# Two bursts of weight spreading in every third slice of an attention and convolution kernel

## The chip, the cores and the metric

The kernel runs on one core of a Trainium2 chip. The metric is the device time of one execution in microseconds, lower is better. TensorE (PE) does the matmuls, VectorE (DVE) elementwise work and reductions, ScalarE (ACT) activations and copies, GpSimd (POOL) elementwise work between SBUF tiles, and SyncE (SP) issues most DMAs.

## The reference

Two layers with a residual each, on x of 16 images of 56 x 56 pixels and 384 channels, all in float32:

```
x = x + attention(group_norm(x))      # layer 0
x = x + depthwise_conv(group_norm(x)) # layer 1

attention: qkv = x @ w_qkv.T; three groups of 128 channels with dilations 1, 2, 3
  for each group, 4 heads of 32 channels, each pixel attends to its 3 x 3 dilated neighbours:
    attn = softmax over 9 of (q . k_neighbour) * 32 ** -0.5
    out  = sum over 9 of attn * v_neighbour
  y = concat(out) @ w_proj.T + b_proj
depthwise_conv: 3 x 3, one filter a channel, weights replaced by their signs (after a clip)
group_norm: 32 groups of 12 channels, over all pixels of an image, no scale or shift
```

## The kernel before

Channels lie on the partitions. The work is cut into 112 chunks (index m): 7 chunks of 8 rows (448 pixels, PX) for each of 16 images. Three planners put the pieces of each chunk on a common clock of slices with `at(when, order, piece)`: `plan_a` turns the input and takes its statistics, `plan_b` is the attention, `plan_c` the convolution. A chunk starts every 9 slices (STEP), so in the steady state each run of nine slices holds the same mixture of pieces of several chunks; the texts call it a round. At the end the pieces are emitted sorted by slice, and within a slice by the order constants of line 833. The framework's scheduler may then still move an instruction past others when it expects it to be ready earlier or later; the buffers of the pools and all waits are derived from the program. Each engine takes its own instructions strictly in the resulting order.

Of `plan_b`, with t0 = 9m, these pieces matter:

- `query(g)` (L483, slices t0-1, t0+2, t0+5): nine 128x448 projections give q of group g in the one bank of `ps_q`.
- `score(i)`, i = 0 to 8 (L509, slice t0+i; i = 3g + ky): VectorE multiplies q with three shifted views of k into a tile t of 3 x 448 (L517). The nine scores of a pixel and head are sums over 32 channels. They are made by matmuls of t with a selection matrix `sel` that is 32 columns wide (L502, tile ps), collected in `ready` and issued in bursts by `score_rounds`: at i = 2 and 5 eight of them, at i = 8 eleven. Each float32 matmul is two instructions in the profile: 16 and 22.
- `softmax_1` to `softmax_5` and `turn_weights` (slices t0+9 to t0+12): transposes (pt_s, L537), maximum, exponent, sum and division on VectorE and ScalarE (L540 to L548), a split of each weight into three bfloat16 terms (ScalarE L556, GpSimd L560, L564, L565), and a DMA that transposes them into aT (L570, on SyncE's queue).
- `weigh(i)`, i = 0 to 8 (L574, slices t0+14+i): three bfloat16 matmuls with 24 rows each (tile pb_a, L583) spread the weights of three neighbours over the 32 channels of their heads into the three banks of `ps_bc`, which has one buffer. The texts call these three a burst, and burst i is that of weigh(i). VectorE multiplies pb_a with three shifted views of v into w (L590). GpSimd adds the second and third w of a group to the first (L598) and then sums the three neighbours into y (L601, L602).
- `out_project(j)` (L608, slices t0+24+j): po from y0, y1, y2 (L616), residual and statistics on VectorE (L619, L622).
- `k_or_v` (L468): pkv (L464), copied by ScalarE (L474), with halo rows copied by DMAs (L478, L479).

Of `plan_c`: three loads make z from x1d (L684), ScalarE normalises z (L697) and zg (L740) and multiplies nine taps for the last group of channels (L769), GpSimd sums them (L776, L782, L785), and `convolve(j)` (L705) does 24 matmul instructions of 96 rows and 32 columns (pc, L711). In the rounds at an image's start the convolution is one slice later. `turn(s)` (pt_o, L792) turns results for the output. Once an image `group_norm` makes statistics by small steps on TensorE, VectorE and GpSimd (L309 to L382).

Most PSUM tiles (pt_x, pkv, po, pt_s, pt_o, pc) share the three buffers of `ps_mt`, so each waits until the tile three before it is read out. `in_one_go` (L289) keeps the matmuls of a burst together.

What fixes the place of the two kinds of bursts is

```
if i % 3 == 2:
    score_rounds(3 if i == 8 else 2)                   
at(t0 + 14 + i, WEIGH, lambda i=i: weigh(i))           
SOFTMAX, SCORE, STATISTICS, CONVOLVE, WEIGH, QUERY, ...
```

Of the kernel before, what the change touches and what calls it, by code (L numbers as in the profile page):

```python
# [35 lines left out]
def dilated_attention_then_binary_conv(  # L36
# [39 lines left out]
    def place(p):  # L76

        g, o = divmod(p, NTAP)
        return NG * o + g
# [201 lines left out]
    def rows(ap):  # L281
        return ap.rearrange("p (r w) -> p r w", w=W)

    def three(t, d, ky):

        tw = t[:, ky * d : ky * d + ROWS, 0:W]
        return bass.AP(tw.tensor, tw.offset, [tw.ap[0], (d, 3), *tw.ap[1:]])

    def in_one_go(matmuls):  # L289

        matmuls[0]()
        with tc.high_priority():
            for m in matmuls[1:]:
                tc.keep_in_program_order(m())
# [97 lines left out]
    def at(when, order, piece):  # L392

        pieces.setdefault((when, order), []).append(piece)
# [51 lines left out]
    def plan_b(m, t0):  # L446
# [44 lines left out]
        def score_rounds(rounds):  # L491

            burst = ready[: rounds * NQ]
            del ready[: rounds * NQ]
            if "ps" not in had:
                had["ps"] = ps_s.tile([P, 512], F32, tag="s", name="ps")

            def add(p, tk):
                j, i = p % NQ, p // NQ
                s0 = SEL0 - 4 * i  # L500
                issued[j] += 1
                return nc.tensor.matmul(  # L502
                    had["ps"][32 * j : 32 * j + 32, :PX], sel[:, s0 : s0 + 32], tk,
                    start=(issued[j] == 1), stop=(issued[j] == len(range(j, NG * NTAP, NQ))),
                )

            in_one_go([lambda a=a: add(*a) for a in burst[-1:] + burst[:-1]])

        def score(i):  # L509

            g, ky = divmod(i, 3)
            d = DIL[g]
            qg = rows(had["q"][:, :PX])
            q3 = bass.AP(qg.tensor, qg.offset, [qg.ap[0], (0, 3), *qg.ap[1:]])
            k3 = three(kv[0][g][m % K_SLOTS], d, ky)
            t = t_p.tile([P, 3, PX], F32, tag="t", name="t")
            nc.vector.tensor_tensor(t.rearrange("p k (r w) -> p k r w", w=W), q3, k3, ALU.mult)  # L517
            ready.extend((i * 3 + kx, t[:, kx, :]) for kx in range(3))
            if i % 3 == 2:
                score_rounds(3 if i == 8 else 2)  # L520

        GH = NG * HEADS
        weights = ew.rearrange("p (s v) -> p s v", s=NSUB)[:, :, :NR]
# [50 lines left out]
        def weigh(i):  # L574

            g, ky = divmod(i, 3)
            pb = ps_bc.tile([P, 3, 512], F32, tag="bc", name="pb_a")

            def copy(kx):
                v = place(3 * i + kx)  # L580
                lo = 32 * (v // 2 % 4)
                rows_of = slice(lo, lo + 2 * TERMS * HEADS)
                return nc.tensor.matmul(  # L583
                    pb[:, kx, :PX].rearrange("p (s n) -> p s n", s=NSUB), spread[rows_of, v % 2, :],
                    had["a"][rows_of, :, v // 8, :], start=True, stop=True
                )

            in_one_go([lambda kx=kx: copy(kx) for kx in (2, 0, 1)])
            w = w_p.tile([P, 3, PX], F32, tag="w", name="w")
            nc.vector.tensor_tensor(  # L590
                w.rearrange("p k (r w) -> p k r w", w=W),
                pb[:, :, :PX].rearrange("p k (r w) -> p k r w", w=W), three(kv[1][g][m % V_SLOTS], DIL[g], ky), ALU.mult,
            )
            if ky == 0:
                had["w0"] = w
                return
            w0 = had["w0"]
            nc.gpsimd.tensor_tensor(w0, w0, w, ALU.add)  # L598
            if ky == 2:
                had[f"y{g}"] = y = y_p.tile([P, PX], F32, tag="y", name="y")  # L600
                nc.gpsimd.tensor_tensor(y, w0[:, 0], w0[:, 1], ALU.add)  # L601
                nc.gpsimd.tensor_tensor(y, y, w0[:, 2], ALU.add)  # L602
# [29 lines left out]
            at(t0 - 1 + 3 * g, QUERY, lambda g=g: query(g))  # L632
        for i in range(9):
            at(t0 + i, SCORE, lambda i=i: score(i))
        at(t0 + 9, SOFTMAX, softmax_1)
        at(t0 + 10, SOFTMAX, softmax_2)
        at(t0 + 11, SOFTMAX, softmax_3)
# [1 line left out]
        at(t0 + 12, SOFTMAX, softmax_5)  # L639
        at(t0 + 12, LOADS, turn_weights)  # L640
        for i in range(9):
            at(t0 + 14 + i, WEIGH, lambda i=i: weigh(i))
        at(t0 + 20, LOADS, load_residual)
        for j in range(NG):
            at(t0 + 24 + j, PROJECT, lambda j=j: out_project(j))
# [184 lines left out]
        for s in range(NSUB):  # L830
            at(t0 + 9 + s, STAGE_C, lambda s=s: turn(s))

    SOFTMAX, SCORE, STATISTICS, CONVOLVE, WEIGH, QUERY, SPREAD, QKV, PROJECT, STAGE_A, STAGE_C, NORM, LOADS = range(13)

    STAT_ORDER = (STATISTICS, SPREAD, SPREAD, SPREAD, STATISTICS, SPREAD)
    STEP = 9
# [45 lines left out]
    for m in range(N):  # L882
        plan_a(m, start_a(m))
        plan_b(m, STEP * m)
        plan_c(m, STEP * (m + 10))
# [31 lines left out]
```

## Time and profile before

| | |
|---|---|
| median of 3 runs | 5253.52 us (5253.09 to 5254.31) |
| span of the profiled execution | 5259.5 us |
| granted TensorE clock | full in nearly all of the span |
| HBM traffic | 466 MB read, 231 MB written |

The page gives the busy time of each engine; the timeline lists instructions in order of time, runs of equal ones merged, with start, length and, in brackets, the idle time of the engine just before and what ended it. Names read out<-in with buffer numbers left out, then the shapes. A float32 matmul has 128x448 in its row and stands twice. A round of nine slices is found by the score sums x22, which come once in it. The queue of SyncE is listed as SPq: its rows are issues, not transfers.

### The profile page before, as it was taken

To read this page: it belongs to the slowest core of one execution; us is meant where nothing else is said; L and a number is where in the kernel's file an instruction comes from. 1 tells how busy PE (TensorE), PEld (TensorE's weight loads), DVE (VectorE), ACT (ScalarE), POOL (GpSimd) and SP (SyncE) were. 2 spreads that over 40 slices of the span, in tenths; PEclk is the share of its full clock that TensorE was granted. 3 is DMA by queue.
4 is the path that set the end of the run, shared out by engine and by line. 5 is a ranking of instruction groups with operands and counts; after the bars stand their busy time and mean duration, and the time that the engine had idled before them with its cause. 6 is when DMAs were issued, how large, how long until landed. Compare 5 with 4: busy or idle time off the path is not lost. (4 is left out here: it accounts for less than half of the span.)

```text
span 5259.5 us, 75515 instructions
## 1 busy us (share of the span) xinstructions
PE 5106.2 (97%) x26885; PEld 2327.2 (44%) x26885; DVE 4188.3 (80%) x4125; ACT 2313.4 (44%) x4077; POOL 4256.5 (81%) x2950
## 2 busy tenths in 40 slices
PE   7999999999999999999999999999999999999976
PEld 4444444444444444444444444444444444444423
DVE  4887888888888888888888878888888888878764
ACT  3223444444444444445444444444445444444443
POOL 2667888888888888888888788888888888898881
PEclk9999999999999999999999999999999999999987
DMA  6434556556555655565665566556565555554545
GB/s 195 126 113 109 165 162 169 158 160 167 156 164 164 170 164 159 163 167 164 161 161 165 151 170 166 160 165 165 165 164 164 161 159 165 141 139 135 136 134 157
DMA packets 811630, 825.62 MB, mean 157 GB/s; under 512 B 360307, under 2 KB 801014, under 8 KB 811254
## 3 DMA queue, kind: packets, MB, share of 16 engines
q1 hardware_dynamic: 803270, 808.79, 56.4%
q10 hardware_dynamic: 7984, 12.00, 0.7%
q8 instruction: 213, 3.49, 0.3%
q14 instruction: 163, 1.34, 0.1%
HBM read 466.41 MB, written 231.21 MB: 133 GB/s over the span
## 5 line engine op out<-in xcount | busy, mean ns | idle before, releaser
L598 POOL TENSOR_TENSOR w<-w 128x1344 f32<-128x1344 f32 x672 | 2075.4, 3088 | 457.0 <-DVE w L590 437.3
L590 DVE TENSOR_TENSOR w<-pb_a,v 128x1344 f32<-128x1344 f32 x1008 | 1554.8, 1542 | 241.3 <-PE pb_a L583 187.6
L517 DVE TENSOR_TENSOR t<-pq,k 128x1344 f32<-128x1344 f32 x1008 | 1536.7, 1551 | 228.7 <-PE pq L464 221.7
L464 PE MATMUL pkv<-xn,wqkvT 128*128 128x448 f32 x3924 | 1566.2, 548 | 0.4 <-DVE xr L619 0.4
L464 PEld LDWEIGHTS pkv<-xn,wqkvT 128*128 128x128 f32 x3924 | 717.5, 190 | 669.8 <-issue 643.4
L616 PE MATMUL po<-y,wprojT 128*128 128x448 f32 x2016 | 838.5, 552 | 56.8 <-POOL y L602 36.1
L697 ACT ACTIVATE z<-z,mrz 96x448 f32<-96x448 f32 x840 | 578.4, 751 | 676.6 <-DMA z<-x1d 407.4
L464 PE MATMUL pq<-xn,wqkvT 128*128 128x448 f32 x1962 | 833.9, 559 | 0.0
L776 POOL TENSOR_TENSOR m<-m 128x1344 f32<-128x1344 f32 x210 | 640.1, 3048 | 151.8 <-ACT m L769 147.6
L502 PE MATMUL ps<-t,sel 128*32 128x448 f32 x6048 | 658.4, 544 | 6.2 <-DVE t L517 5.3
L769 ACT ACTIVATE m<-zg,ktap 128x448 f32<-128x448 f32 x945 | 555.6, 659 | 16.5 <-POOL m L776 6.8
L616 PEld LDWEIGHTS po<-y,wprojT 128*128 128x128 f32 x2016 | 377.4, 192 | 417.8 <-issue 336.5
L711 PE MATMUL pc<-z,kdiag 96*32 96x440 f32 (+1 forms) x5040 | 514.0, 541 | 6.5 <-POOL z L699 4.4
L464 PEld LDWEIGHTS pq<-xn,wqkvT 128*128 128x128 f32 x1962 | 344.3, 189 | 318.1 <-issue 318.1
L619 DVE SCALAR_TENSOR_TENSOR xr<-po,bias,xr 128x448 f32<-128x448 f32 x336 | 228.6, 680 | 235.9 <-PE po L616 231.9
L602 POOL TENSOR_TENSOR y<-y,w 128x448 f32<-128x448 f32 x336 | 381.5, 1136 | 16.3
L601 POOL TENSOR_TENSOR y<-w 128x448 f32<-128x448 f32 x336 | 381.7, 1136 | 13.7
L474 ACT COPY v<-pkv 128x448 f32<-128x448 f32 x336 | 176.3, 525 | 483.8 <-PE pkv L464 466.1
L583 PE MATMUL pb_a<-aT,spread 24*128 24x448 bf16 x3024 | 368.4, 359 | 21.2 <-DMA aT<-e 10.9
L718 DVE TENSOR_TENSOR x<-pc,x 128x448 f32<-128x448 f32 x224 | 138.5, 618 | 272.1 <-PE pc L711 269.2
L474 ACT COPY k<-pkv 128x448 f32<-128x448 f32 x336 | 178.9, 532 | 377.7 <-PE pkv L464 377.7
L583 PEld LDWEIGHTS <-spread 24*128 24x128 bf16 x3024 | 98.3, 91 | 510.3 <-issue 489.2
(132 smaller groups left out, 4280.4 us busy)
## 6 DMA issues: line engine op xcount, KB each, us to landing
z<-x1d SPq DMA_DIRECT2D x570, 224.0 KB, 3.9
xr<-xd SPq DMA_DIRECT2D x112, 672.0 KB, 4.2
x1d<-xr SPq DMA_DIRECT2D x112, 672.0 KB, 3.2
xn<-xd SPq DMA_DIRECT2D x109, 672.0 KB, 4.6
xin<-in_x_dram SPq DMA_DIRECT2D x105, 672.0 KB, 7.5
xd<-xa SPq DMA_DIRECT2D x315, 224.0 KB, 3.4
out_dram<-osb SPq DMA_DIRECT2D x420, 168.0 KB, 3.5
x<-x1d SPq DMA_DIRECT2D x112, 448.0 KB, 8.3
```

Of the source, the lines that this page charges most:

```text
L464: nc.tensor.matmul(dst[:, :PX], wqkvT[:, cc, o0 : o0 + P], had["xn"][:, cc, :], start=(cc == 0), stop=(cc == NG - 1))
L502: return nc.tensor.matmul(had["ps"][32 * j : 32 * j + 32, :PX], sel[:, s0 : s0 + 32], tk, start=(issued[j] == 1), stop=(issued[j] == len(r ...
L517: nc.vector.tensor_tensor(t.rearrange("p k (r w) -> p k r w", w=W), q3, k3, ALU.mult)
L583: return nc.tensor.matmul(pb[:, kx, :PX].rearrange("p (s n) -> p s n", s=NSUB), spread[rows_of, v % 2, :], had["a"][rows_of, :, v // 8, :] ...
L590: nc.vector.tensor_tensor(w.rearrange("p k (r w) -> p k r w", w=W), pb[:, :, :PX].rearrange("p k (r w) -> p k r w", w=W), three(kv[1][g][m ...
L598: nc.gpsimd.tensor_tensor(w0, w0, w, ALU.add)
L601: nc.gpsimd.tensor_tensor(y, w0[:, 0], w0[:, 1], ALU.add)
L616: nc.tensor.matmul(po[:, :PX], wprojT[:, g, j * P : (j + 1) * P], had[f"y{g}"], start=(g == 0), stop=(g == NG - 1))
L697: nc.scalar.activation(z, z, AF.Identity, bias=mrz[:, j, q, 0:1], scale=mrz[:, j, q, 1:2])
L711: return nc.tensor.matmul(pcr[q * HD : (q + 1) * HD, :, lo:hi], kdiag[:, kx, j * NQ + q, :], rows(set_of(j, q))[:, :, lo + kx - 1 : hi + k ...
L769: nc.scalar.activation(rows(t[:, kx]), zp[:, ky : ky + ROWS, kx : kx + W], AF.Copy, scale=ktap[:, o : o + 1])
L776: nc.gpsimd.tensor_tensor(had["m"], had["m"], t, ALU.add)
```

## The change

It takes the bursts of score sums out of `score(i)` and plans them on their own, with an order constant BURST right behind SCORE. It gives three of the nine `weigh` pieces (i = 0, 3, 6) an order WEIGH_AHEAD between SCORE and BURST, and plans i = 1, 4, 7 one slice earlier, where they keep the order WEIGH. So slices t0+14, t0+17 and t0+20 hold two weigh pieces each, with the score sums, the statistics and the convolution planned between them; the slices after them hold none, and those after that one (i = 2, 5, 8), as before. The computation is the same.

```diff
@@ in score(i)
             ready.extend((i * 3 + kx, t[:, kx, :]) for kx in range(3))
-            if i % 3 == 2:
-                score_rounds(3 if i == 8 else 2)
@@ at the end of plan_b
         for i in range(9):
             at(t0 + i, SCORE, lambda i=i: score(i))
+            if i % 3 == 2:
+                at(t0 + i, BURST, lambda i=i: score_rounds(3 if i == 8 else 2))
...
         for i in range(9):
-            at(t0 + 14 + i, WEIGH, lambda i=i: weigh(i))
+            pair = i % 3
+            at(t0 + 14 + i - (pair == 1), WEIGH_AHEAD if pair == 0 else WEIGH, lambda i=i: weigh(i))
@@ order within a slice
-    SOFTMAX, SCORE, STATISTICS, CONVOLVE, WEIGH, QUERY, SPREAD, QKV, PROJECT, STAGE_A, STAGE_C, NORM, LOADS = range(13)
+    (SOFTMAX, SCORE, WEIGH_AHEAD, BURST, STATISTICS, CONVOLVE, WEIGH, QUERY, SPREAD, QKV, PROJECT, STAGE_A, STAGE_C,
+     NORM, LOADS) = range(15)
```

## The prediction

> **What bounds the kernel now.** I read the busy times first, then the waits of TensorE, then TensorE's timeline over one ordinary round of nine slices, and last the places where VectorE and GpSimd meet.
>
> ```profile
> PE 5106.2 (97%) x26885; PEld 2327.2 (44%) x26885; DVE 4188.3 (80%) x4125; ACT 2313.4 (44%) x4077; POOL 4256.5 (81%) x2950
> ```
> TensorE is busy for 97% of the span. Its matmul spans overlap, so I go by start-to-start distances, which repeat to the hundredth.
>
> ```profile
> 2505.21 0.60 PE L537 MATMUL pt_s<-perm,sT 128*112 128x128 f32 x4
> 2505.74 0.36 PE L583 MATMUL pb_a<-aT,spread 24*128 24x448 bf16 x3
> 2506.04 4.78 PE L464 MATMUL pkv<-xn,wqkvT 128*128 128x448 f32 x12
> ...
> 2525.73 1.71 PE L502 MATMUL ps<-t,sel 128*32 128x448 f32 x16
> 2527.25 2.41 PE L711 MATMUL pc<-z,kdiag 96*32 96x448 f32 x24
> 2529.60 0.36 PE L583 MATMUL pb_a<-aT,spread 24*128 24x448 bf16 x3
> 2529.90 2.52 PE L464 MATMUL pq<-xn,wqkvT 128*128 128x448 f32 x6
> 2532.35 0.36 PE L583 MATMUL pb_a<-aT,spread 24*128 24x448 bf16 x3
> 2532.64 4.78 PE L464 MATMUL pkv<-xn,wqkvT 128*128 128x448 f32 x12
> 2537.26 2.42 PE L616 MATMUL po<-y,wprojT 128*128 128x448 f32 x6
> 2539.61 0.36 PE L583 MATMUL pb_a<-aT,spread 24*128 24x448 bf16 x3
> 2539.90 2.52 PE L616 MATMUL po<-y,wprojT 128*128 128x448 f32 x6
> 2542.36 2.46 PE L502 MATMUL ps<-t,sel 128*32 128x448 f32 x22
> 2544.74 0.36 PE L583 MATMUL pb_a<-aT,spread 24*128 24x448 bf16 x3
> ```
> No row here has an idle note: one round (2497.91 to 2542.36) takes 44.45 us with no gap, so only TensorE's own pitches and new waits can move it. A burst (three pb_a matmuls) occupies 0.29. Six full-array matmuls take 2.45 between two bursts (2529.90 to 2532.35), 2.35 with a burst on one side (2537.26 to 2539.61) and, at 2502.96 in the same timeline, 2.25 with none. So entering a burst costs the neighbour 0.10 and leaving it 0.10: a burst inside full-array work costs 0.49, of which 0.20 is change of shape.
>
> ```profile
> 2378.19 1.71 PE L502 MATMUL ps<-t,sel 128*32 128x448 f32 x16
> 2379.83 1.02 PE L464 MATMUL pq<-xn,wqkvT 128*128 128x448 f32 x2
> ```
> ```profile
> 4603.32 0.36 PE L583 MATMUL pb_a<-aT,spread 24*128 24x448 bf16 x3
> 4603.61 1.71 PE L502 MATMUL ps<-t,sel 128*32 128x448 f32 x16
> ```
> Sixteen score sums take 1.52 before a convolution (also 32 columns wide) and 1.64 before full-array work: leaving that shape costs 0.12. A burst straight into score sums costs its 0.29 and nothing more.
>
> What TensorE waits for in the whole run is small:
> ```profile
> PE po L616 <- ACT v L474: 20.3, 28, 1.9
> PE pb_a L583 <- DMA aT<-e: 10.9, 8, 2.1
> PE pb_a L583 <- DVE w L590: 10.2, 7, 2.0
> ```
> And one place where VectorE is held while GpSimd works:
> ```profile
> 2343.99 6.20 POOL L598 TENSOR_TENSOR w<-w 128x1344 f32<-128x1344 f32 x2
> 2347.51 2.70 DVE L345 TENSOR_SCALAR var<-var 32x2 int32<-32x2 int32 x1
> ```
> A shift over 32x2 numbers takes 2.70 us and ends at 2350.21, with the GpSimd add (2350.19).
>
> **What the Trainium skill says.** "TensorEngine Tiling (Array Packing)", Key Properties: changing the tiling mode, not just the tile, drains TensorE. The trace agrees, at 0.10 to 0.12 us a change, except into score sums from a burst (none seen). "SBUF — State Buffer", Who interferes with whom: VectorE in a mode that takes both ports, and GpSimd, lock each other out for a whole instruction. The 2.70 us shift agrees; the multiplies of L590 read PSUM and show no such stretch (1483 to 1560 ns over 1008).
>
> **The change part by part.** I take the order of instructions from the built changed program. Burst i is weigh(i). Per round TensorE now has: score sums 22, burst 4, pq, po, pt_s, pkv, pt_x, pt_o, burst 5, pt_o, score sums 16, convolution, burst 6, pq, burst 7, pt_x, pt_o, pkv, pt_o, burst 8, pt_x, score sums 16, burst 0, convolution, burst 1, pq, pkv, po, burst 2, po, burst 3. So it does what it says in two of three slices; in the slice with burst 6 the convolution still stands ahead of both, the pq between them. No instruction is added or removed, no DMA belongs to a moved step; the score sums stay behind the same products.
>
> 1. *Shapes.* Before: 6 bursts inside full-array work (6 x 0.20), 3 from 32-column into full work (3 x 0.22), 3 entries into score sums (3 x 0.10): 2.16. After: 4 x 0.20, 3 x 0.22, po-burst-score sums 0.10, two other entries 0.20, and score sums-burst-convolution. That last one has no row: from below 0, since leaving a shape could hide; from above 0.30, two full drains and an entry. I take 0.14 (0.12 out of the score sums, 0.02 in). Sum 1.90: a gain of 0.26 a round. The convolution runs in 102 of 112 rounds: 26.5 us (bounds 11 to 41). The first ten rounds lose two enclosed bursts, 0.4 each: 4 us.
>
> 2. *Second burst of a pair.* All bursts write the same three PSUM banks, so it waits for VectorE's multiply of the first. Behind the waiting burst stand all later matmuls; behind the multiply, VectorE's queue. Burst 3 to 4: VectorE has the residual add (starts 2.57 after its po, 2542.47 for 2539.90), the multiply 0.60 later, 1.55 long: done 4.72 after po starts. Burst 4 is due after 2.45 + 0.29 + 2.38 = 5.12: margin 0.40. Burst 0 to 1: multiply done 0.49 + 1.55 = 2.04, due 0.29 + 2.37: margin 0.6. Burst 6 to 7: convolution's add first, done 2.23, due 0.29 + 2.45: margin 0.5. Where the convolution comes late (15 rounds) four pq matmuls and half a pt_x lie between: due 2.19, margin 0.15. Cost 0, hidden behind those matmuls; uncovered it is the missing time once a pair.
>
> 3. *Statistics rounds.* There VectorE's order is now multiply 8, the shift L345, multiply 0, convolution's add, multiply 1. From burst 8 on: multiply 8 ends at 2.03 (2344.97 to 2347.00), its GpSimd add holds the shift until 5.24, multiply 0 ends at 6.8. Burst 1 is due at 0.29 + 0.29 (statistics) + 0.53 + 1.64 + 0.29 + 2.37 = 5.41. Wait 1.4, in the 12 rounds with a long shift (33.2 us over 14 shifts, 2.7 each): a loss of 17. Bounds 0 (the shift slips in between two GpSimd adds) and 25.
>
> 4. *Turned weights.* Slice 0 of a round has lost its burst, so VectorE reaches the softmax division one multiply (1.5) sooner, and GpSimd's order now does the three-part split (1.16 + 0.6 + 1.15) ahead of the add of burst 5 (3.05) and two y adds (2.27). The transposing DMA, issued at 2522.94 with 4.0 to landing in the ordinary round, goes some 5 us earlier, while burst 0 needs it only 2.35 sooner (one convolution). The 10.9 us of waits for aT go.
>
> 5. *SyncE.* In before's order the transposing DMA blocks the queue from 2516.6 to 2522.94, and the loads of z and xg behind it; z lands at 2531.48, ScalarE normalises z (2.72), zg, six taps (3.47) and only then copies v (2538.85 to 2539.37), for which the second po waits (2539.90: margin 0.53). Shapes alone would take 0.49 of that margin (two bursts gone between convolution and po, one change left). With the queue free sooner the z loads go 3 to 4 us and xg some 2.5 us earlier; two more taps stand ahead of v (1.2). Net 1.3 earlier: the margin grows. Of the 20.3 us of waits on v I take 16 as gone; bounds 20 gone, or 10 added if xg lands as late as before.
>
> 6. *GpSimd and the end.* Its adds come earlier or at the same time; y2 stays 4.7 ahead of po. The last 200 us are bound by adds that are the same: 0, within 5 either way.
>
> Sum: -26.5 - 4 + 17 - 10.9 - 16 = -40; I keep 4 for small misses of margin (15 rounds at 0.15): -36 on the span of 5259.5. The median 5253.5 stands 6 below that execution; the difference carries over: 5217.
>
> **Rivals.** *Slower, through the shared PSUM banks:* the multiply of a pair's first burst is late by more than the margins of part 2. With lateness d beyond my times, the loss is 306 pairs x (d - 0.5); against -36 it turns at d = 0.62. For: TensorE's lead grows as its own time shrinks, and 10.2 us of such waits exist already. Against: VectorE idles 8.5 of 44.45 us a round, and the multiply never stretches. At d = 0.75: 5294. *Shapes only:* loads and v are no earlier, parts 4 and 5 give a third: -26.5 - 4 + 17 - 9 = -22, with some extra waits on v 5240. *No change:* what shapes give, waits on multiplies take, 0.3 a round: 5253.
>
> **How the numbers follow.** Main 0.56 (own range 5198 to 5236), shapes only 0.18 (two thirds of it beyond 0.2%), no change 0.10, slower 0.16. About 0.2%, 10.5 us, is what a measurement of this kernel can tell from none. Faster: 0.56 + 0.12 = 0.68; same 0.16; slower 0.16. The range 5196 to 5262 leaves out the slower case and a little below.
>
> **What would show it.** Ordinary round 44.18 instead of 44.45; pb_a waits on the multiply near 17 us more, all in the statistics rounds; no wait on aT in the body; waits of po on v under 6 us; transposing DMA ahead of the z load. Wrong if score sums-burst-convolution costs over 0.4, or if burst 4, 1 or 7 waits in ordinary rounds.

## The result, and the profile after

| | before | after |
|---|---|---|
| median of 4 runs each | 5253.92 us (5253.09 to 5254.78) | 5222.21 us (5220.73 to 5226.85) |
| ratio, 95% interval | | 0.9941 (0.9927 to 0.9955) |
| span of the profiled execution | 5259.5 us | 5221.6 us |
| ordinary round | 44.44 us | 44.14 us |
| round with statistics (12 of them) | 47.13 us | 48.47 us |
| TensorE waits for the multiply of the burst before | 10.2 us, 7 times | 36.7 us, 31 times |
| waits of po for v | 20.3 us, 28 times | none |

The change saves 31.7 us in the medians; the result lies 5.2 us above the forecast of 5217. The busy line of the changed kernel's page shows TensorE with 20.5 us less of busy time for the same instructions:

```profile
PE 5085.7 (97%) x26885; PEld 2322.5 (44%) x26885; DVE 4199.0 (80%) x4125; ACT 2310.7 (44%) x4077; POOL 4242.2 (81%) x2950
```

This is one ordinary round in TensorE's timeline (start and duration in us, the engine, line, operation, tiles):

```profile
2477.13 0.60 PE L535 MATMUL pt_s<-perm,sT 128*112 128x128 f32 x4
2477.57 4.68 PE L464 MATMUL pkv<-xn,wqkvT 128*128 128x448 f32 x12
...
2497.11 1.71 PE L502 MATMUL ps<-t,sel 128*32 128x448 f32 x16
2498.75 0.36 PE L581 MATMUL pb_a<-aT,spread 24*128 24x448 bf16 x3
2499.05 2.44 PE L712 MATMUL pc<-z,kdiag 96*32 96x448 f32 x24
2501.42 0.36 PE L581 MATMUL pb_a<-aT,spread 24*128 24x448 bf16 x3
```

The next pt_s starts at 2521.27, 44.14 us on, and no row has an idle note. Slice 0 has no burst any more between pt_s and pkv. The sequence that had no row before is there: score sums to burst 1.64 (1.52 straight into a convolution), burst 0.30, convolution to the next burst 2.37 (2.35 before). So beyond the burst itself it costs 0.12 + 0.02, the 0.14 that was taken.

TensorE waits in the changed kernel for these (reason, us in total, times, longest):

```profile
PE pb_a L581 <- DVE w L588: 36.7, 31, 2.4
...
PE pb_a L581 <- DMA aT<-e: 5.9, 3, 4.4
...
PE pkv L464 <- ACT xa L435: 3.5, 12, 0.3
```

The waits of po on v are not in the list at all. Of those on aT, one of 0.8 us is in the first round that spreads weights and the two others (4.4 and 0.7) are near the end. One wait of 6.4 us of pt_x for v, at 475.9, stands where the kernel before waited 6.2 us for y (505.1). New are the twelve waits of pkv for xa, and most of those for the multiply.

Twelve of the multiply waits are alike, one in each statistics round. The round at 2315 us shows how they arise; the lines are of VectorE, GpSimd and TensorE in turn:

```profile
2315.57 1.56 DVE L588 TENSOR_TENSOR w<-pb_a,v 128x1344 f32<-128x1344 f32 x1 [0.93 <-POOL dev L333]
...
2317.65 2.63 DVE L345 TENSOR_SCALAR var<-var 32x2 int32<-32x2 int32 x1
...
2320.39 1.56 DVE L588 TENSOR_TENSOR w<-pb_a,v 128x1344 f32<-128x1344 f32 x1
```
```profile
2317.21 3.05 POOL L596 TENSOR_TENSOR w<-w 128x1344 f32<-128x1344 f32 x1 [2.53 <-DVE var L342]
```
```profile
2317.86 0.36 PE L581 MATMUL pb_a<-aT,spread 24*128 24x448 bf16 x3
...
2322.01 0.37 PE L581 MATMUL pb_a<-aT,spread 24*128 24x448 bf16 x3 [1.42 <-DVE w L588]
```

Burst 0 starts at 2317.86 and takes 0.29, so its multiply could have begun by about 2318.3 (an estimate: below, without the held shift, a multiply starts 0.48 us after its burst). It begins at 2320.39, behind a shift of 32x2 numbers that lasts until GpSimd's add is over (2317.21 + 3.05 = 2320.26). The second burst of the pair waits 1.42 us, and so does everything behind it on TensorE.

The table gives the profiled times by stretch, from the last score sums of one round to those of a later one, in us:

| stretch | before | after | difference |
|---|---|---|---|
| up to the first | 94.5 | 92.3 | -2.2 |
| the next 14 rounds | 594.6 | 580.0 | -14.6 |
| 84 rounds of the body | 3796.3 | 3771.8 | -24.5 |
| 13 rounds of the last two images | 571.7 | 580.5 | +8.8 |
| the end | 202.4 | 197.0 | -5.4 |

### The profile page after: what moved, and what is told of

Its sections match the earlier page's. It is cut to its first block, busy times and chain, and to the rows that moved or that the text cites. A ratio compares the mean times of both kernels' runs of the same rounds, so it can differ in the third digit from the quotient of the medians.

```text
span 5221.6 us, 75614 instructions
## 1 busy us (share of the span) xinstructions
PE 5085.7 (97%) x26885; PEld 2322.5 (44%) x26885; DVE 4199.0 (80%) x4125; ACT 2310.7 (44%) x4077; POOL 4242.2 (81%) x2950
## 5 line engine op out<-in xcount | busy, mean ns | idle before, releaser
L596 POOL TENSOR_TENSOR w<-w 128x1344 f32<-128x1344 f32 x672 | 2048.7, 3049 | 327.3 <-DVE w L588 279.1
L464 PE MATMUL pkv<-xn,wqkvT 128*128 128x448 f32 x3924 | 1542.2, 542 | 3.9 <-ACT xa L435 3.5
L614 PE MATMUL po<-y,wprojT 128*128 128x448 f32 x2016 | 834.9, 550 | 17.3 <-POOL y L600 17.3
L777 POOL TENSOR_TENSOR m<-m 128x1344 f32<-128x1344 f32 x210 | 639.1, 3044 | 43.3 <-ACT m L770 37.9
L435 ACT COPY xa<-pt_x 128x448 f32<-128x448 f32 x315 | 167.4, 534 | 618.2 <-PE pt_x L423 618.2
L558 POOL TENSOR_TENSOR rest<-ew,e 112x512 f32<-112x512 f32 x112 | 130.1, 1162 | 358.9 <-ACT e L554 358.9
L581 PE MATMUL pb_a<-aT,spread 24*128 24x448 bf16 x3024 | 369.5, 360 | 42.7 <-DVE w L588 36.7
```

Source lines behind the costliest of these rows:

```text
L464: nc.tensor.matmul(dst[:, :PX], wqkvT[:, cc, o0 : o0 + P], had["xn"][:, cc, :], start=(cc == 0), stop=(cc == NG - 1))
L581: return nc.tensor.matmul(pb[:, kx, :PX].rearrange("p (s n) -> p s n", s=NSUB), spread[rows_of, v % 2, :], had["a"][rows_of, :, v // 8, :] ...
L614: nc.tensor.matmul(po[:, :PX], wprojT[:, g, j * P : (j + 1) * P], had[f"y{g}"], start=(g == 0), stop=(g == NG - 1))
L777: nc.gpsimd.tensor_tensor(had["m"], had["m"], t, ALU.add)
```

## The experiments

Each ratio is to runs of the kernel before that were timed along with it; their medians were 5251.5 to 5254.2 us. Of the code, only the lines that differ are shown.

### The shift in PSUM

```
-ri = r.bitcast(I32)
-nc.vector.tensor_single_scalar(ri, v.bitcast(I32), 1, op=ALU.arith_shift_right)
-nc.vector.tensor_scalar(ri, ri, -1, RSQRT_BITS, op0=ALU.mult, op1=ALU.add)
+ri, pi = r.bitcast(I32), pv[:GN_G, 8 : 8 + L]
+nc.vector.tensor_scalar(pi, pv[:GN_G, 0:L], 1.0 / GN_CH, 1e-5, op0=ALU.mult, op1=ALU.add)
+nc.vector.tensor_single_scalar(pi.bitcast(I32), pi.bitcast(I32), 1, op=ALU.arith_shift_right)
+nc.vector.tensor_scalar(ri, pi.bitcast(I32), -1, RSQRT_BITS, op0=ALU.mult, op1=ALU.add)
```

> The changed kernel, with the variance's shift reading and writing PSUM: VectorE computes v a second time into an unused part of pv's bank (one instruction of about 0.14 us more, 14 times), shifts it there and reads it there for the last step; the arithmetic is the same. Theory (the shift is held by GpSimd's add [...], and so is the multiply behind it): the shift takes about 0.14 us instead of 2.63, the twelve waits of a burst for the multiply in the statistics rounds (1.42 us each) go, those rounds go from 48.47 to about 47.05, and the time from 5222 to about 5205. Rival (the shift waits for something else of GpSimd, such as a result that is late): the instruction moves nothing, the round stays at 48.5 and the time at 5222.

Measured: 5206.21 us (ratio 0.9908, 0.9893 to 0.9923), statistics round 46.98. These are VectorE and TensorE at the same place of this kernel (its line numbers are one higher):

```profile
2311.19 0.14 DVE L346 TENSOR_SCALAR pv<-pv 32x2 int32<-32x2 int32 x1
...
2311.81 1.56 DVE L589 TENSOR_TENSOR w<-pb_a,v 128x1344 f32<-128x1344 f32 x1 [0.30 <-PE pb_a L582]
```
```profile
2311.33 0.36 PE L582 MATMUL pb_a<-aT,spread 24*128 24x448 bf16 x3
...
2313.99 0.36 PE L582 MATMUL pb_a<-aT,spread 24*128 24x448 bf16 x3
```

The shift takes 0.14 us and VectorE waits for the burst, not the burst for VectorE. In all 18 uses it lasts 137 to 155 ns. The second burst follows the first after 2.66 us, with no wait. In the Trainium skill, "SBUF — State Buffer", Who interferes with whom, VectorE and GpSimd exclude each other only on the SBUF ports that they share; the run agrees, for with both operands in PSUM the hold is gone. That it costs the changed kernel 16 us is shown.

### The same in the kernel before

This is the same edit, made on the kernel before.

> The kernel before, with the variance's shift in PSUM as in the run above. Theory (there the held shift had cover, since burst 1 came one full-array stretch later): the shift falls from 2.70 to 0.14 us, and the time stays: 5254, statistics round 47.1. Rival (the hold cost the kernel before too, so that what the PSUM shift brought is no loss of the change): 5254 - 17 = 5237.

Measured: 5252.84 us, ratio 1.000 (0.9992 to 1.0008), statistics round 47.14. The shift is short there too (139 ns at the median, 2700 before), and nothing is gained. So the hold was covered, and the change took the cover away: there burst 0 stood behind the convolution (2.35 us) and burst 1 behind six full-array matmuls more, so that the hold was over when their multiplies were due.

### One pair alone, and the other two

For the first, only bursts 3 and 4 pair up; for the second only 0 and 1, and 6 and 7:

```
-pair = i % 3
+pair = i % 3 if i // 3 in (1,) else 2
```
```
-pair = i % 3
+pair = i % 3 if i // 3 in (0, 2) else 2
```

> Only the pair of bursts 3 and 4 is moved; bursts 0, 1, 6, 7 stand as in the kernel before. By my prices this is nearly all of the gain: one burst fewer inside full-array work (0.20 a round over 112 rounds, 22 us), the softmax and the transposing DMA earlier (aT waits, 11 us, gone), the waits on v (20 us) mostly gone; and none of the loss in the statistics rounds, since burst 0 and burst 1 lie apart again. The last image's waits (9 us) stay. Ordinary round 44.24, statistics rounds 46.9 to 47, time about 5209, that is faster than the whole change. Rival (each of the three moved bursts brings a third): 5243, and 44.34 for the ordinary round.

> Only the pairs 0 and 1, and 6 and 7 are moved; burst 4 keeps its place behind the score transposes. By my prices: burst 1 straight behind the convolution saves 0.20 and costs 0.14, burst 7 saves nothing, so the ordinary round is 44.38; the statistics rounds are longer by the wait of 1.4; aT and its DMA come no earlier, so the 11 us of aT waits stay, and the waits on v stay or grow (a burst fewer between convolution and po). Time 5254 - 6 + 17 + (0 to 10) = 5265 to 5275. Rival (each moved burst brings a third of the gain): 5233, ordinary round 44.24.

Measured: pair 3 and 4 alone 5211.90 us (0.9921, 0.9908 to 0.9935), ordinary round 44.25, statistics round 46.94. The other two pairs alone took 5286.60 us (1.0057, 1.0044 to 1.0069; its runs go from 5274 to 5288), ordinary round 44.33, statistics round 48.66. The profile of the second is of its fastest run, 13 us under its median, so it does not show the whole loss. Its waits:

```profile
PE po L614 <- ACT v L474: 23.9, 25, 2.2
...
PE pb_a L581 <- DMA aT<-e: 11.1, 8, 2.1
```

The moved burst 4 alone beats the whole change. The shift is held there too (2.7 us, 13 times), and no burst of a statistics round waits for it; with the other two pairs alone, twelve waits of 1.2 to 1.3 us are back. The other two save 0.11 us an ordinary round, but leave the waits on v and aT as they were and bring the wait in the statistics rounds; their image-start rounds also grew (46.1 to 48.4, against 44.9 to 46.9 before). The gains of shape add up: 0.19 + 0.11 = the 0.30 of the whole. The times do not (-42 and +32 against -32). With pair 3 and 4 moved, the waits on v and aT are small, with the others moved or not; that this is the whole of the difference is not shown.

### Bursts in the same slices, without an order of their own

```
-at(t0 + 14 + i - (pair == 1), WEIGH_AHEAD if pair == 0 else WEIGH, lambda i=i: weigh(i))
+at(t0 + 14 + i - (pair == 1), WEIGH, lambda i=i: weigh(i))
```

> The bursts go into the same slices as in the change, but each pair's first burst has no place of its own ahead of the score sums and the convolution. The program then has score sums, burst 3, pq, burst 4, po; score sums, convolution, burst 0, pq, burst 1. So the order no longer saves a change of shape, but slice 0 has lost its burst between po and the key and value projections, and the softmax comes earlier. By my prices: ordinary round 44.4 (against 44.14 and 44.44); aT waits (11 us) and the waits on v (16 to 20 us) gone; no wait of 1.4 in the statistics rounds, since pq lies between burst 0 and burst 1; last images about as in the change. Time 5254 - 4 - 30 + 3 + (0 to 9) = 5223 to 5232. Rival (the gain is one of shapes alone): 5250 to 5254.

Measured: 5313.17 us (1.0123, 1.0107 to 1.0139). The ordinary round is 44.40 as expected, so without the order there is next to no gain of shape. The rest of the expectation fell. Its waits:

```profile
PE po L614 <- ACT v L474: 28.0, 26, 2.5
PE pv L339 <- POOL dev L333: 23.4, 14, 2.8
```

Those on aT are 13.7 us. Most of the loss lies in the statistics rounds (48.7 to 50.7 us), where the matmul of the variance now waits for GpSimd's dev, and in the image-start rounds (46.2 to 49.3).

VectorE's timeline of an ordinary round (pt_s starts at 2532.66) shows why the weights are late again. The multiply of burst 4 now precedes the softmax and does not hold it up: the maximum starts 0.98 us after pt_s, against 1.48 in the change. But a second product, and the multiply of burst 5 (2539.83), stand ahead of the division.

```profile
2531.58 1.55 DVE L588 TENSOR_TENSOR w<-pb_a,v 128x1344 f32<-128x1344 f32 x1
...
2533.64 0.60 DVE L538 TENSOR_REDUCE mx<-pt_s 112x48 f32<-112x432 f32 x1
...
2541.24 0.60 DVE L546 TENSOR_TENSOR ew<-ew,sm 112x432 f32<-112x432 f32 x1
```

In the change (pt_s starts at 2477.13) the same two steps are closer:

```profile
2478.61 0.60 DVE L538 TENSOR_REDUCE mx<-pt_s 112x48 f32<-112x432 f32 x1
...
2483.05 0.61 DVE L546 TENSOR_TENSOR ew<-ew,sm 112x432 f32<-112x432 f32 x1
```

The next table gives medians over the ordinary rounds, read from the timelines: the time from pt_s to the end of the division and to the issue of the transposing DMA, and how long before the second po its v has been copied. The last two columns are the waits of the whole run, all in us.

| kernel | division ends | DMA issued | v copied ahead of po | waits on v | waits on aT |
|---|---|---|---|---|---|
| before | 9.7 | 17.6 | 0.8 | 20.3 | 10.9 |
| bursts 1 and 7 moved | 9.7 | 17.6 | 0.5 | 23.9 | 11.1 |
| no order of their own | 9.2 | 17.1 | 0.5 | 28.0 | 13.7 |
| burst 4 moved | 7.0 | 10.9 | 3.1 | 2.6 | 2.0 |
| the change | 6.5 | 10.4 | 3.2 | 0 | 5.9 |

The kernels fall into two groups. An empty slice is not enough. What stands on VectorE between the maximum and the division sets when the weights are ready: one product in the change, two products and a multiply where the bursts have no order of their own. No run moved the DMA alone in SyncE's queue, so that its place there, and not the softmax as such, frees v, is an inference from these rows.

### The waits in the last two images

In the last two images the next images' first stage is missing. There the program has burst 6 straight behind the score sums, ahead of the convolution, and burst 6 waits for the multiply of burst 5. These are VectorE, GpSimd and TensorE of the changed kernel at the first such place:

```profile
4590.69 2.79 DVE L546 TENSOR_TENSOR ew<-ew,sm 112x432 f32<-112x432 f32 x1
```
```profile
4589.97 3.05 POOL L596 TENSOR_TENSOR w<-w 128x1344 f32<-128x1344 f32 x1
```
```profile
4590.91 1.71 PE L502 MATMUL ps<-t,sel 128*32 128x448 f32 x16
4595.00 0.37 PE L581 MATMUL pb_a<-aT,spread 24*128 24x448 bf16 x3 [2.39 <-DVE w L588]
```

The division, 0.6 us in most rounds, is held by the add until 4593.02 and takes 2.79; the multiply of burst 5 starts behind it (4593.41).

```
-pair = i % 3
+pair = i % 3 if i // 3 == 1 or b < B - 2 else 2
```

> The changed kernel, but in the last two images bursts 1 and 7 stand as in the kernel before (burst 4 stays moved). There the order differs: with no first stage left to interleave, the changed program puts burst 6 straight behind the score sums, ahead of the convolution, 2.4 us sooner than elsewhere. Theory (it is this place that makes burst 6 wait for the multiply of burst 5, in front of which the softmax division stands): the waits on the multiply in the last 14 rounds (8.6 us) go, these rounds fall from 580.5 to about 571.5, and the time from 5222 to about 5213; the statistics rounds keep their 1.42. Rival (the waits belong to the thinner TensorE work of the last images as such): they stay, 5222.

Measured: 5221.63 us (0.9942, 0.9928 to 0.9956). The 13 rounds fall to 571.9 as expected, the statistics rounds keep 1.42, and the time doesn't move: the end, 197.0 us with the whole change, takes 204.7 (202.4 before). Of the waits on the multiply in these 13 rounds about half stay, in other places (4.5 of 9.0 us). The last rounds and the end behave as one stretch, 777.5 us with the whole change and 776.6 here: what is taken from one place comes back as a wait of po for GpSimd's y (26.2 us, longest 11.6, against 17.3 and 5.9 in the changed kernel). The place of the waits was right, their price was not.

### The division on GpSimd

```
-nc.vector.tensor_tensor(by_neighbour(weights), by_neighbour(weights), over_neighbours(sm), ALU.mult)
+nc.gpsimd.tensor_tensor(by_neighbour(weights), by_neighbour(weights), over_neighbours(sm), ALU.mult)
```

> The changed kernel, with the softmax division (ew<-ew,sm 112x432) on GpSimd instead of VectorE. Theory (the waits of the last image and of three image starts come from the division, which now falls into a GpSimd add and is held until its end, and with it the multiply of burst 5): the waits pb_a on the multiply outside the statistics rounds (8.6 us in the last image, 3.7 at 144, 1142 and 2399 us) go, and the 1.42 in each statistics round stay: 5222 - 10 = about 5212. On GpSimd the division is estimated at 1.0 us (a subtraction over 112x512 takes 1.16 there), which the idle time ahead of the split (3.3 us in an ordinary round) takes up. Rival (those waits come from VectorE's load as such, or GpSimd has no room): 5222 or above, up to 5235.

Measured: 5224.07 us (0.9943, 0.9931 to 0.9956). This missed the expected 5212, and it tells little: the scheduler made another program of it. Burst 6 went ahead of the convolution in ordinary rounds (44.25), in the statistics rounds the multiply of burst 0 went ahead of the shift, whose wait is gone (46.88), and the first 14 rounds took 589.8 and the last 13 588.7. What the held division costs by itself stays open.

### The variance one slice earlier

```
-STAT_SLICE = (0, 1, 2, 4, 5, 7)
+STAT_SLICE = (0, 1, 2, 3, 5, 7)
```

> The changed kernel, with the variance step one slice earlier (the shift as it was, in SBUF). VectorE then has, between the shift and the multiply of burst 0, a product and a statistics instruction, and burst 0 comes later, behind the score transposes' neighbour. Theory (what counts is whether burst 1 is due before a held shift and the multiply behind it are done): the shift is still held (about 2 to 3 us), no burst waits 1.42 for it, statistics round 47 to 47.3, time about 5205. Rival (any held shift in this stretch costs its 2.6 us, or the earlier variance finds GpSimd's sums not ready): statistics round 48.5 or more, 5222 or more.

Measured: 5298.95 us (1.0091, 1.0076 to 1.0106), statistics rounds 52.8 to 54.2. The shift is short now (146 ns, before the add starts), but the second part of the rival came true; the largest of TensorE's waits:

```profile
PE pv L339 <- POOL dev L333: 48.2, 15, 4.3
```

The matmul of the variance comes before GpSimd has made dev, and the whole array waits for six tiny matmuls (3.2 us in the round at 2346 us). Nothing about the hold follows from it.

### Towards a version that beats both

The first try has the shift in PSUM, with the last two images' bursts 1 and 7 as before:

> The variance's shift in PSUM and the last two images' bursts 1 and 7 as before, together. If the two losses are separate, 5206 - 9 = about 5197, faster than both kernels: ordinary round 44.14, statistics round 46.98, last 14 rounds (13 of them timed) 571.5. Rival (the losses share their cover, and one gives back what the other brings): 5206.

Measured: 5203.96 us (0.9908, 0.9894 to 0.9922), against 5206.21 with the PSUM shift alone, a difference within the intervals. The rounds of the last images are 571.0, and the end takes it back again (207.7).

The second has the shift in PSUM, with burst 7 left where it was in all images:

```
-pair = i % 3
+pair = i % 3 if i // 3 in (0, 1) else 2
```

> The change with the variance's shift in PSUM, but burst 7 stands as in the kernel before (burst 1 and burst 4 stay moved). By my prices burst 7's move saves nothing, since it lies inside full-array work in both places, and it cost 0.29 us in each statistics round, where it no longer stands between the last transposes and the key and value projections. So the ordinary round stays at 44.14, the statistics round goes from 46.98 to about 46.69, the waits of the projections on xa (3.5 us) go, the time from 5206 to about 5202. Rival (burst 7's place carries a share of the saved shape changes): ordinary round 44.2 or more, 5206 to 5212.

Measured: 5201.74 us (0.9904, 0.9888 to 0.9921), the lowest of all, some 20 us below the change and 50 below the kernel before; the intervals do not tell it apart from the run above. Statistics round 46.88, image-start rounds 44.72 (44.87 with the change), no wait of pkv for xa. But the ordinary round is 44.19, so burst 7's move had saved 0.05, not nothing. Its TensorE timeline:

```profile
2526.64 0.36 PE L582 MATMUL pb_a<-aT,spread 24*128 24x448 bf16 x3
2526.94 4.78 PE L465 MATMUL pkv<-xn,wqkvT 128*128 128x448 f32 x12
2531.55 0.38 PE L794 MATMUL pt_o<-ident,x 128*112 128x128 f32 x2
```

pkv takes 4.61 behind a burst and 4.51 without (2477.57 to 2482.08 in the change), while the four transposes pt_x take 0.43 behind a burst and 0.39 without: a burst that is followed by transposes costs about half as much to leave.

## Why the prediction was right, and where it was not

The forecast was right in what gains and what loses: fewer changes of shape, earlier weights and v, and the held shift in the statistics rounds. Term by term it was this.

- *Shapes.* Forecast 0.26 a round, measured 0.30. The terms: burst 4 0.20 taken, 0.19 measured; burst 1 0.06 taken (0.20 saved less the 0.14), 0.06 measured (44.25 to 44.19); burst 7 0 taken, 0.05 measured. Over the body it is 72 rounds without statistics x 0.30 = 21.6.
- *Second burst of a pair.* No second burst waits in an ordinary round of the body, as forecast. Missed: the margins were worked out for the order of the body, and for a division of 0.6 us. In the last two images burst 6 stands ahead of the convolution; the waits of 0.4 us and more there are eight, 8.6 us in all. In four other rounds a burst waits 0.5 to 2.3, once behind a held shift and three times behind a held division. The price was small in the end, since the last stretch gives or takes the same elsewhere.
- *Statistics rounds.* 1.4 in 12 rounds, 17 us forecast; 1.42 and 17.0 measured. The PSUM shift gives 16 back in the change and nothing in the kernel before, so cause and lost cover are both shown. Missed: the 0.29 in the same rounds, 3.5 us. With burst 7 gone from between the last transposes and pkv, pkv comes before ScalarE has emptied its buffer (xa); with burst 7 back in its place the wait is gone, and with bursts 1 and 7 moved alone the same twelve are there.
- *Turned weights.* Five of the waits on aT (9.0 us) were in the first rounds, and all in the body are gone. With 14 of those rounds 14.6 us shorter, this and the 4 us of shapes account for nearly all of that stretch. Not forecast were 4.4 and 0.7 us of new aT waits near the end.
- *SyncE.* 16 of 20.3 us of waits on v forecast as gone, all are. The kernel before has the transposing DMA between its z loads, the change has it first (the first three rows are before, the other two after):

```profile
2516.23 0.32 SPq L684 DMA_DIRECT2D z<-x1d  x1
2522.94 1.41 SPq L570 DMA_TRANSPOSE aT<-e  x1
...
2526.53 0.43 SPq L684 DMA_DIRECT2D z<-x1d  x1
```
```profile
2487.54 1.54 SPq L568 DMA_TRANSPOSE aT<-e  x1
2489.17 1.68 SPq L685 DMA_DIRECT2D z<-x1d  x2
```

  The copies of v in the same rounds, before and after:

```profile
2538.85 0.52 ACT L474 COPY v<-pkv 128x448 f32<-128x448 f32 x1
```
```profile
2506.92 0.51 ACT L474 COPY v<-pkv 128x448 f32<-128x448 f32 x1
```

  The forecast's direction was right and its sizes too small: counted from pt_s, ScalarE starts on z 5.8 us sooner where the loads were put 3 to 4 earlier, and v is ready 3.9 sooner, not 1.3. So its margin ahead of po grows from 0.53 to 3.80 in these rounds.
- *GpSimd and the end.* The forecast was 0, within 5; it was +8.8 in the last rounds and -5.4 at the end, 3.4 together. It held for a reason that it did not give: the new waits of the last rounds are mostly given back at the end.
- *The sum.* -36 forecast, -37.9 in the profiled executions. That is so close in part by luck: shapes and v gave some 3 and 4 us more than taken, and xa (3.5) and the last stretch (3.4), which were put at nothing, took as much. The medians lie only 31.7 apart, and that is the step where the 5 us were lost: the difference of one profile was carried over to the median whole. A run's time is some 1.7 us more than its span, so the profiled execution of before was some 7 above its median, that of after 1 above. A second profile of the kernel before, with its PSUM shift and the same median, has a span of 5249.8. Its waits on v and aT are only 2.5 us less in all (18.0 and 10.7), so what makes the rest of the 10 us between these two executions stays open.

The rival of shared PSUM banks came true in the twelve statistics rounds, in the four rounds named above and in the last two images, not in the body at large; "shapes only" fell with the waits on v.

## What to carry to other kernels

When two uses of one buffer are drawn together, list what else the engine between them does in *every* kind of round, the rare ones and the last ones too: here the ordinary round had forecast margins of 0.4 us and more, and the loss came from a shift of 32x2 numbers in one round of seven. Price each moved piece alone: one of three moves alone brought more than the whole change, the other two brought a small gain of shape and the loss. A small VectorE instruction with its operands in SBUF can last until the GpSimd instruction beside it ends (2.6 us for 0.14 here); moving its operands to PSUM removed that for one more tiny instruction. It is worth doing only where something waits for it: the same move gained 16 us in one order and nothing in the other.

## What the runs showed of the hardware beyond that

A division with both inputs in SBUF (112x432, 0.6 us alone) is held by a GpSimd add as well, up to 3.36 us, and ends some 0.46 us after it; the Trainium skill, "SBUF — State Buffer", Who interferes with whom, says so of VectorE instructions with two SBUF inputs, and the trace agrees. The multiplies with one input in PSUM stay at 1494 to 1559 ns through 1008 instructions of the changed kernel. The add that holds another keeps its 3.05 us. The other way about it is the add that is held: in the kernel before, all of the 107 adds (of 672) that start while a division runs take 3.26 us or more, and none of the others does; in the changed kernel only two adds start so.

Entering or leaving the 24-row bursts has no single price: 0.10 to full-array matmuls on each side, 0.04 into transposes (0.43 against 0.39), 0.02 into the convolution (2.37 against 2.35), nothing seen into score sums.
